# A residual block in fp32 on one core: bias added while VectorE empties the bank for tiles 18 to 27, four more warming products, and a new hand order

## The chip, the cores and the metric

The kernel runs on one core of a Trainium2 chip. The metric is device time in microseconds, the median of the runs shown. The engines are TensorE (PE, with its weight loads listed as PEld), VectorE (DVE), ScalarE (ACT), GpSimd (POOL) and SyncE (SP), whose queue issues nearly all DMAs. Matrix products write PSUM banks of 128 x 512 fp32; everything else lies in SBUF.

## The reference

Inputs are x (4, 1024, 512), cond (4, 256), W (1536, 512) and b (512), all fp32:

```python
hidden = jnp.concatenate([cond, cond], axis=-1)
x_mean = jnp.mean(x, axis=1, keepdims=True)
fused = jnp.concatenate([x, x_mean * ones_L, hidden[:, None, :] * ones_L], axis=-1)
out = x + jax.nn.relu(jnp.einsum('bld,do->blo', fused, W) + b)
```

So out = x + relu(x W0 + bias_r). W0 is the first third of W, and bias_r = mean_r W1 + hidden_r W2 + b is one row of 512 numbers for each of the four batch rows r.

## The kernel before, in words

**Tiles and products.** Batch and length give 32 tiles of 128 x 512; tiles 8r to 8r+7 belong to batch row r. fp32 is split: x and W0 are each cut into a high part (`hi`, `w_hi`, fp32r) and a low part (`lo`, `w_lo`), and a tile is 12 products 128x128 by 128x512: four blocks j of the contraction, times hi·w_hi (n=0), lo·w_hi (n=1) and hi·w_lo (n=2). A task `p5.3` issues all three n of tile 5, block 3; `p0.1.2` issues one. The 32 tiles have 384 products; tile 31 is done in two halves of 256 columns (`l` and `r`). The product is line 365.

**Getting x transposed.** x comes twice. For tiles 0 to 3 the plain rows (`X0.0` tile 0, `X0.1` tile 1, `X0.2` tiles 2 and 3) are regrouped (`y`, lines 236 and 238) and turned by TensorE (`T0` to `T2`, line 260). For the other tiles, in units of four (unit u holds tiles 4u-8 to 4u-5), a load with 512-byte pieces (`Z`) is turned by VectorE (`T`, line 262). ScalarE then makes `hi` and the row sums (`h`, line 269), and VectorE or GpSimd make `lo` (`l`, line 275; for odd j both inputs lie in SBUF, for even j one is a PSUM bank). Plain x is also loaded (`X`) for the residual.

**The bias row.** When all sums of a batch row r are there, GpSimd makes the mean (`to`), ScalarE puts the condition part into the bank `acc` (`as`), VectorE adds four terms (`m`, line 319), the halves are folded (`f`, `fa`), split (`vh`, `vl`, line 339), multiplied with ones on TensorE (`pb`, line 343), and ScalarE copies it out (`bc`, line 347). No tile of row r can get its bias before `bc`r.

**Emptying a bank.** Five banks `po` take the tiles in turn (tile t uses bank t mod 5, the left half of tile 31 bank 1, the right half bank 2). `WAYS` gives each tile one of three ways:

- K: ScalarE or VectorE copies the bank into a buffer `o` (`K`, lines 430 and 432); later GpSimd or VectorE add the bias (`b`, line 436), ScalarE or VectorE clip (`r`, lines 447 and 445), and GpSimd or VectorE add x (`F`, line 454).
- B: VectorE adds the bias while it empties the bank into `o` (`K`, line 440); then `r` and `F` as above.
- I: ScalarE writes the bias into the bank before the tile's first product (`P`, line 419; lines 399 and 403 for tile 31); the products add to it; VectorE clips and adds x in one instruction straight from the bank (`F`, line 423).

So tile t+5 may begin, in ways K and B, when `K`t is done; in way I it also waits for its own `P`, which waits for the emptying. There are 12 buffers `o`: the thirteenth tile that uses one waits for the `F` of the first.

**The order.** Nothing is scheduled automatically. `ORDER` (lines 22 to 49) is one list of task names, and each engine executes its own tasks strictly in that list's order; `@d`, `@a`, `@p` put a task on VectorE, ScalarE or GpSimd. A store `S` and the loads `X`, `Z`, `M`, `V`, `C`, `B` are issued in list order by SP, and a store waits in that queue for its `F`. `W0` and `W1` go through ScalarE's queue. `fill` (line 133) is a product of zeros (128x128 by 128x512 bf16) whose result nobody reads; there are seven, all before the first real product.

Of the kernel before, what the change touches and what calls it, by code (L numbers as in the profile page):

```python
# [19 lines left out]
ORDER = """
W0@a fill W1@a X0.0 X0.1 W2 fill relu fill W3 fill X0.2 fill Z3.3 fill y0.0@a T0.0 fill y1.0@d y1.1@p h0.0 y0.2@d
y0.1@p l0.0@d T0.2 T0.1 T1.0 T1.1 wh0r@a wh0l@d Z3.0 T1.2 T1.3 T0.3 h1.0 p0.0.1 h0.1 wh1@d C p1.0.0 h1.1 p0.0.0
l0.1@d h0.3 Z3.2 p1.1.0 wl1@p l1.0@d h0.2 p0.1.1 wh2@d Z3.1 h1.3 p0.1.0 l0.3@d h1.2 p1.0.1 l0.2@d p0.2.0 wh3@a
l1.1@d p1.2.0 wl2@d V p0.2.1 p0.3.0 wl3@p B p1.1.2 l1.2@d p0.3.1 Z4.2 y3.0@a y2.0@d p0.1.2 wl0r@d p1.2.2 p1.2.1
wl0l@p l1.3@d p1.1.1 T2.2 Z4.3 T2.3 p0.2.2 h2.3 T2.0 T2.1 h2.2 l2.3@d p1.3.2 h2.1 p1.3.0 l2.2@d Z4.1 p3.3 h2.0 Z4.0
l2.0@d p2.3 t0 l2.1@d p3.2 t3 p2.0 T3.3 p0.0.2 p0.3.2 T3.1 p3.0 h3.3 T3.0 K0@a p1.3.1 l3.3@p p2.1 t1 h3.0 T3.2 M2
p2.2 l3.0@d M1 h3.2 ac0@p p3.1 M3 h3.1 p1.0.2 p5.3 M0 K2@a K1@d to0 p4.3 Z5.3 l3.1@d ac1@p p5.0 Z5.0 t2 p4.0 l3.2@d
g0.0 p4.1 K3@d g0.1 Z5.2 d0.0 p6.3 p6.1 T4.3 Z5.1 d0.1 p4.2 T4.1 T4.0 p5.2 K4@a Z6.2 T4.2 as0 p7.1 g1.0 p5.1 Z6.0  # L30
h4.0 d1.0 p7.2 h4.3 l4.0@d p6.2 Z6.3 h4.2 m0.0 l4.3@p p7.0 K5@a m0.1 h4.1 p9.0 Z6.1 m0.2 g1.1 l4.1@p p6.0 m0.3 g2.0
Z7.2 p10.3 l4.2@d f0 d1.1 p7.3 fa0 Z7.1 p9.3 K7@a T5.2 d2.0 g2.1 p8.3 T5.0 Z7.0 vh0 p8.0 T5.1 d2.1 h5.0 p9.2 K6@d
h5.2 Z7.3 p8.2 T5.3 h5.1 vl0 p9.1 g3.1 X4.0 l5.1@p l5.2@d X1.0 p10.0 h5.3 l5.0@d p10.1 Z8.0 l5.3@p T6.0 p11.3 T6.2
Z8.1 to1 pb0 p8.1 T6.3 bc0@a T6.1 as1 p10.2 b0@p K9@a m1.0 p12.2 Z9.3 K8@a m1.1 p11.2 b1@p h6.0 m1.2 h6.3 p14.2 m1.3
h6.2 b3@p p12.1 r0@a l6.2@d p11.1 r1@a l6.0@d l6.3@p p13.2 K10@a h6.1 p11.0 f1 l6.1@p p15.3 r3@a fa1 p15.2 K11@a
T7.3 F1@p p15.1 vh1 T7.2 h7.3 p15.0 T7.0 F0@p h7.2 S1 p12.3 Z8.2 vl1 h7.0 p14.0 Z9.0 T7.1 F3@p Z8.3 p16.3 b2@d X5.0
h7.1 X4.1 pb1 p16.0 Z9.1 bc1@a to2 as2 p13.3 l7.3@p S0 K15 Z9.2 g3.0 p16.1 m2.0 b4@p X3.0 p13.1 m2.1 p14.3 m2.2 X1.1
b5@p r4@a p12.0 m2.3 p13.0 f2 X3.1 K12 l7.1@p r2@a p16.2 fa2 p14.1 K13 vh2 F4@p r5@a p17.3 vl2 p17.0 l7.0@d F2@p S4
T8.0 X2.1 pb2 p17.2 bc2@a d3.0 S2 P18 p17.1 K16 X5.1 h8.0 p18.1 T8.3 d3.1 P21 p18.0 T8.1 X2.0 K14 p18.2 h8.1 l7.2@d
p21.3 P19 X6.0 T8.2 h8.3 p21.1 l8.0@d as3 l8.3@p p19.0 S3 P20 T9.0 p19.1 h8.2 l8.1@p T9.3 p21.0 h9.0 l8.2@d h9.3  # L40
p18.3 F5@p T9.2 p20.3 T9.1 h9.2 p19.3 F18 S5 h9.1 p21.2 K17 P23 to3 p19.2 P22 b7@p m3.0 p20.2 r17@a m3.1 r12@a p22.1
b6@p m3.2 r16@a p23.3 m3.3 p22.3 l9.3@p F19 f3 p20.0 r7@a X7.0 fa3 p20.1 S19 r14@a X6.1 vh3 p23.0 F14@p vl3 p23.2
l9.2@d p23.1 F12@p b9@d pb3 p22.0 bc3@a F7@p r13@d P24 p22.2 F23 p24.0 F22 p24.3 F20 S22 P27 p24.2 S7 P28 r9@d S18
F21 p24.1 F9@p P25 S14 l9.0@d r6@a S20 p27.1 P26 F6@d F17@p p28.2 p27.3 b11@d b10@p S17 p26.3 S21 p26.0 l9.1@d S6
F13@p r10@a S9 p27.2 F24 p26.1 F16@p r11@d S24 p27.0 b8@d S23 p26.2 S12 F11@p X7.1 p28.3 F26 p25.0 S11 F27 P31l S26
P29 p25.1 S13 r15@a p25.2 P31r F15@p p29.2 p28.0 p25.3 p29.1 F25 p31.3r r8@d S25 P30 p29.3 F8@p S15 p31.2r S16
p31.0r S27 p30.1 F10@p S8 p28.1 p31.1r p29.0 F31r S31r p30.0 F29 S10 p31.3l F28 S29 p30.3 S28 p30.2 p31.0l F30
p31.2l p31.1l S30 F31l S31l
""".split()


# [437 lines left out]
```

## Time and profile before

| | |
|---|---|
| runs | 106.45 us median of 3 (105.53 to 107.67) |
| profiled execution | 106.27 us |
| its span, first to last instruction | 104.5 us |
| instructions | 1424 |
| PE / DVE / ACT / POOL busy | 97.6 / 79.1 / 59.1 / 70.1 us |
| data moved | 27.36 MB, 262 GB/s over the span |

All times inside the span are counted from its first instruction. The profiled execution's own time is 1.77 us longer than its span. "Idle before" in a row is the time that the engine waited just ahead of the instruction, and the name behind the arrow is what released it. Matmuls overlap their neighbours, so their durations do not add up; what counts is the distance from one start to the next.

### The profile page before, as it was taken

The numbers are of one execution on the slowest core, as the hardware profiler recorded it, in microseconds if no ns is written. First come the engines' busy times: TensorE is split into PE (matmuls) and PEld (weight loads), VectorE is DVE, ScalarE is ACT, GpSimd is POOL, SyncE is SP. The second block draws the span as 40 slices with busy tenths as digits, with TensorE's granted clock in tenths as the row PEclk, the third lists the DMA queues.
The fourth block names the chain that finished last, engine by engine and source line by source line (L and its number), as shares of the span: only waits on it lengthen the run. The fifth ranks groups of instructions, "written<-read, shape, count | busy, mean of one in ns | idle before, by whom it ended". The sixth has DMA issues, their size and how long they took to land.

```text
span 104.5 us, 1424 instructions
## 1 busy us (share of the span) xinstructions
PE 97.6 (93%) x423; PEld 76.6 (73%) x423; DVE 79.1 (76%) x129; ACT 59.1 (57%) x148; POOL 70.1 (67%) x69
## 2 busy tenths in 40 slices
...
GB/s 62 328 350 217 233 236 270 181 195 267 219 231 237 246 223 221 322 205 148 259 286 315 263 377 387 409 396 151 20 140 401 384 369 173 289 348 404 296 272 146
DMA packets 25345, 27.36 MB, mean 262 GB/s; under 512 B 1397, under 2 KB 15993, under 8 KB 25338
## 3 DMA queue, kind: packets, MB, share of 16 engines
...
q14 instruction: 4, 0.03, 0.1%
...
## 4 chain that ended last, share of the span: by engine, by line
PE 44%; DVE 22%; DMA 16%; ACT 7%; issue 4%; POOL 4%; SPq 1%; DVEq 0%; POOLq 0%
PE po L365 41%; DMA z<-in_x_dram 9%; DVE acc L319 6%; DMA x<-in_x_dram 4%; DVE xT L262 3%; DMA out_dram<-x 3%; DVE px L262 3%; DVE x L423 2%; DVE lo L275 2%; ACT po L419 2%; ACT hi L269 2%; DVE x L454 2%; DVE o L436 2%; ACT o L447 1%; POOL lo L275 1%
## 5 line engine op out<-in xcount | busy, mean ns | idle before, releaser
L365 PE MATMUL po<-w_hi,hi 128*128 128x512 f32 (+1 forms) x132 | 51.1, 393 | 1.5 <-ACT po L419 1.5
L365 PE MATMUL po<-w_hi,lo 128*128 128x512 f32 (+1 forms) x132 | 51.1, 389 | 0.0
L365 PE MATMUL po<-w_lo,hi 128*128 128x512 f32 (+1 forms) x132 | 50.1, 385 | 0.0
L365 PEld LDWEIGHTS po<-w_hi,hi 128*128 128x128 f32 x132 | 25.3, 192 | 8.2 <-ACT po L419 3.2
L365 PEld LDWEIGHTS po<-w_hi,lo 128*128 128x128 f32 x132 | 25.1, 190 | 5.2 <-DVE lo L275 0.4
L365 PEld LDWEIGHTS po<-w_lo,hi 128*128 128x128 f32 x132 | 24.8, 188 | 5.0
L454 POOL TENSOR_TENSOR x<-o,x 128x512 f32<-128x512 f32 x17 | 23.4, 1396 | 6.6 <-DVE o L445 4.5
L275 POOL TENSOR_TENSOR lo<-xT,hi 128x512 fp32r<-128x512 f32 x12 | 15.5, 1299 | 9.4 <-ACT hi L269 8.1
L319 DVE SCALAR_TENSOR_TENSOR acc<-w_mean,tot,acc 128x512 f32<-128x512 f32 x16 | 12.1, 754 | 1.1 <-DMA w_mean<-in_L_cond_W_dram 0.4
L275 DVE TENSOR_TENSOR lo<-px,hi 128x512 fp32r<-128x512 f32 (+2 forms) x20 | 11.5, 587 | 1.4 <-ACT hi L269 1.3
L269 ACT ACTIVATE hi<-px 128x512 fp32r<-128x512 f32 (+2 forms) x20 | 10.3, 521 | 3.8 <-PE px L260 2.1
L423 DVE SCALAR_TENSOR_TENSOR x<-po,x 128x512 f32<-128x512 f32 x13 | 8.5, 678 | 4.1 <-PE po L365 4.1
L262 DVE STREAM_TRANSPOSE xT<-z 128x512 f32<-128x512 f32 x14 | 9.3, 684 | 3.1 <-POOL cond L301 2.4
L269 ACT ACTIVATE hi<-xT 128x512 fp32r<-128x512 f32 x14 | 8.8, 631 | 3.8 <-DVE xT L262 3.8
L447 ACT ACTIVATE o<-o 128x512 f32<-128x512 f32 x14 | 8.3, 623 | 4.2 <-POOL o L436 4.2
L436 POOL TENSOR_TENSOR o<-o,bias 128x512 f32<-128x512 f32 x8 | 10.7, 1353 | 0.0
L419 ACT ACTIVATE po<-bias 128x512 f32<-128x512 f32 x13 | 7.5, 590 | 5.1 <-DVE x L423 5.0
L262 DVE STREAM_TRANSPOSE px<-z 128x512 f32<-128x512 f32 x14 | 9.4, 700 | 1.0 <-DMA z<-in_x_dram 0.6
L297 ACT ACTIVATE term<-wc,cT 128x512 f32<-128x512 f32 x8 | 5.6, 719 | 2.2 <-POOL tot L309 1.4
L301 POOL TENSOR_TENSOR cond<-b_sb,term 128x512 f32<-128x512 f32 x4 | 5.2, 1302 | 1.4 <-ACT term L297 1.4
L432 ACT ACTIVATE o<-po 128x512 f32<-128x512 f32 x9 | 5.2, 594 | 1.5 <-PE po L365 1.5
L301 POOL TENSOR_TENSOR cond<-cond,term 128x512 f32<-128x512 f32 x4 | 5.2, 1294 | 0.3
...
## 6 DMA issues: line engine op xcount, KB each, us to landing
...
```

Of the source, the lines that this page charges most:

```text
L262: nc.vector.transpose(xT.rearrange("p (n q e) -> p n q e", q=Q // E, e=E), zs[z_of(u)][:, : n * NQ].rearrange("p n (q j e) -> p n j q e", ...
L269: nc.scalar.activation(his[buf][:, col : col + m], xT, AF.Copy, accum_out=sums[:, r, j, s : s + 1])
L275: nc_of[e].tensor_tensor(los[buf][:, col : col + m], xT, his[buf][:, col : col + m].bitcast(F32), ALU.subtract)
L297: nc.scalar.activation(terms[k], wc[:, k], AF.Copy, scale=cT[:, k, r : r + 1])
L301: nc.gpsimd.tensor_tensor(conds[r % 2], conds[r % 2] if k else b_sb, terms[k], ALU.add)
L319: nc.vector.scalar_tensor_tensor(acc, w_mean[:, j, :], tot[:, r, j : j + 1], acc, ALU.mult, ALU.add)
L365: nc.tensor.matmul(v, lhsT=a[:, col : col + P], rhs=m, start=WAYS[t] != "I" and key not in done, stop=done.count(key) == 3 * J - 1, skip_g ...
L419: nc.scalar.activation(bank(t), biases[r], AF.Copy)
L423: nc.vector.scalar_tensor_tensor(x_tile(t), bank(t), 0.0, x_tile(t), ALU.max, ALU.add)
L436: nc_of[e].tensor_tensor(o, o, biases[r], ALU.add)
L447: nc.scalar.activation(o, o, AF.Relu)
L454: nc_of[e].tensor_tensor(x_tile(t), o, x_tile(t), ALU.add)
```

## The change

Three edits. `WAYS` turns tiles 18 to 27 from I to B, so that only tiles 28 to 31 keep I. `fill` writes bank `ps_o[2]` (first used by tile 2) where it wrote `acc` (used to turn tile 1). `ORDER` is written anew, with 11 `fill` where 7 were.

```diff
-WAYS = "KKKKKKKKKKKKBBBBBBIIIIIIIIIIIIII"
+WAYS = "KKKKKKKKKKKKBBBBBBBBBBBBBBBBIIII"
...
     def fill():
         nc.tensor.matmul(
-            acc, lhsT=warm, rhs=warm.rearrange("p (o d) -> p o d", o=1).to_broadcast([P, 4, P]),
+            ps_o[2], lhsT=warm, rhs=warm.rearrange("p (o d) -> p o d", o=1).to_broadcast([P, 4, P]),
             start=True, stop=True,
         )
```

Of `ORDER`, the beginning, the stretch around `pb2`, and the end, first as it was:

```diff
-W0@a fill W1@a X0.0 X0.1 W2 fill relu fill W3 fill X0.2 fill Z3.3 fill y0.0@a T0.0 fill y1.0@d y1.1@p h0.0 y0.2@d
-y0.1@p l0.0@d T0.2 T0.1 T1.0 T1.1 wh0r@a wh0l@d Z3.0 T1.2 T1.3 T0.3 h1.0 p0.0.1 h0.1 wh1@d C p1.0.0 h1.1 p0.0.0
-l0.1@d h0.3 Z3.2 p1.1.0 wl1@p l1.0@d h0.2 p0.1.1 wh2@d Z3.1 h1.3 p0.1.0 l0.3@d h1.2 p1.0.1 l0.2@d p0.2.0 wh3@a
-l1.1@d p1.2.0 wl2@d V p0.2.1 p0.3.0 wl3@p B p1.1.2 l1.2@d p0.3.1 Z4.2 y3.0@a y2.0@d p0.1.2 wl0r@d p1.2.2 p1.2.1
-wl0l@p l1.3@d p1.1.1 T2.2 Z4.3 T2.3 p0.2.2 h2.3 T2.0 T2.1 h2.2 l2.3@d p1.3.2 h2.1 p1.3.0 l2.2@d Z4.1 p3.3 h2.0 Z4.0
...
-b5@p r4@a p12.0 m2.3 p13.0 f2 X3.1 K12 l7.1@p r2@a p16.2 fa2 p14.1 K13 vh2 F4@p r5@a p17.3 vl2 p17.0 l7.0@d F2@p S4
-T8.0 X2.1 pb2 p17.2 bc2@a d3.0 S2 P18 p17.1 K16 X5.1 h8.0 p18.1 T8.3 d3.1 P21 p18.0 T8.1 X2.0 K14 p18.2 h8.1 l7.2@d
...
-F13@p r10@a S9 p27.2 F24 p26.1 F16@p r11@d S24 p27.0 b8@d S23 p26.2 S12 F11@p X7.1 p28.3 F26 p25.0 S11 F27 P31l S26
-P29 p25.1 S13 r15@a p25.2 P31r F15@p p29.2 p28.0 p25.3 p29.1 F25 p31.3r r8@d S25 P30 p29.3 F8@p S15 p31.2r S16
-p31.0r S27 p30.1 F10@p S8 p28.1 p31.1r p29.0 F31r S31r p30.0 F29 S10 p31.3l F28 S29 p30.3 S28 p30.2 p31.0l F30
-p31.2l p31.1l S30 F31l S31l
```

and as it is written:

```diff
+W0@a fill W1@a X0.0 X0.1 W2 fill relu fill W3 fill X0.2 fill Z3.1 fill y0.1@d y0.0@p y0.2@p fill T0.0 wh0r@d Z3.2
+T0.1 T0.2 wh0l@d h0.0 fill wl0r@p fill y1.0@d y1.1@a T0.3 l0.0@d fill h0.2 wl0l@p fill h0.1 T1.2 T1.0 p0.0.1 T1.1
+wh1@d Z3.3 T1.3 p0.0.0 h1.0 p0.0.2 Z3.0 h1.3 l1.0@d p1.0.2 wl1@p h1.2 l0.1@d p1.0.0 l1.3@d wh2@a p0.1.0 p1.0.1 wh3@d
+h1.1 p0.1.1 p0.2.0 h0.3 l0.2@d wl2@p C p1.2.0 l1.1@d p1.3.1 V p0.3.0 p1.1.0 B y3.0@d y2.0@a p1.3.0 p0.2.1 Z4.0
+l1.2@d p1.1.1 wl3@d p1.1.2 p0.2.2 T2.2 Z4.2 T2.3 p1.2.1 h2.2 T2.0 T2.1 l2.2@d p0.3.2 Z4.3 h2.0 p1.2.2 p3.2 h2.3
...
+l7.3@p T7.1 p17.0 b5@d h7.1 p19.3 b9@p h7.0 p17.3 r4@a l7.0@d p19.2 to2 g3.1 l7.2@d F4@p p16.2 r5@a m2.0 p18.3 K15
+b8@p S4 p18.2 Z9.1 m2.1 p16.3 X3.1 d3.1 m2.2 p19.0 m2.3 p18.1 F5@p T8.0 p16.1 f2 fa2 p20.3 b11@p S5 T8.3 S2 p17.2
+vh2 X3.0 h8.0 vl2 p17.1 F6@p X2.1 h8.3 S3 T8.2 p19.1 l7.1@d b7@p S6 p20.0 X4.0 pb2 S0 p18.0 bc2@a l8.3@p X7.0 h8.2
...
+p25.1 S9 r16@a vl3 p25.2 r19@a F16@p r23@d p26.0 l9.0@d p25.3 F19@p S16 pb3 X7.1 p26.3 bc3@a S17 F12@p P28 p27.1 K25
+p27.2 l9.2@d P30 F18@p p28.2 F14@d r25@a p30.2 l9.1@p K26 p28.0 S14 S18 F25@d P31l p27.0 S19 F23@p r26@a p30.0 K24
+S25 p31.2l F26@p S23 K27 p31.0l r24@a S12 p31.1l P29 p31.3l F20@p p30.3 P31r F31l F22@d S31l p29.1 S26 p28.1 S20
+r27@d S22 p29.0 F24@d F27@p p28.3 p29.3 F28 S24 p30.1 S27 S28 p29.2 F30 p31.1r F29 S30 p31.0r p31.3r S29 p31.2r F31r
+S31r
```

By task, with the engine that does it:

| task | before | after |
|---|---|---|
| `fill`, PE | 7 | 11 |
| `P`, ACT | 15 | 5 |
| `r`, ACT / DVE | 14 / 4 | 26 / 2 |
| `K`, DVE / ACT | 9 / 9 | 18 / 10 |
| `F` of way I, DVE (tile 31 has two) | 15 | 5 |
| `F` of ways K and B, POOL / DVE | 17 / 1 | 22 / 6 |
| `b`, POOL / DVE | 8 / 4 | 10 / 2 |
| `l`, POOL / DVE | 12 / 28 | 13 / 27 |

## Rows read from the trace of the kernel before

**Rows 1.** The page's first part: busy us (share of the span) x instructions.

```profile
PE 97.6 (93%) x423; PEld 76.6 (73%) x423; DVE 79.1 (76%) x129; ACT 59.1 (57%) x148; POOL 70.1 (67%) x69
```

**Rows 2.** Windows of 20 us: busy PE, PEld, DVE, ACT, POOL; then clock, DMA.

```profile
40.00:60.00 20.00, 19.77 (x87) 15.79 (x86) 19.36 (x30) 16.12 (x37) 19.62 (x20) 1.00 1.04 254
60.00:80.00 20.00, 19.91 (x85) 15.46 (x84) 17.97 (x27) 13.56 (x32) 14.02 (x13) 1.00 0.78 279
```

**Rows 3.** Timeline of PE, steady stretch: start us, us, what.

```profile
20.42 0.39 PE L365 MATMUL po<-w_hi,hi 128*128 128x512 f32 x1
...
29.48 0.39 PE L365 MATMUL po<-w_hi,lo 128*128 128x512 f32 x1
```

**Rows 4.** Timeline of PE, the start.

```profile
5.65 0.47 PE L260 MATMUL po<-term,o 128*128 128x128 f32 x1 [0.83 <-DVE o L238]
...
8.91 0.57 PE L365 MATMUL po<-w_hi,lo 128*128 128x512 f32 x1
9.32 0.39 PE L365 MATMUL po<-w_hi,hi 128*128 128x512 f32 x1
9.55 0.40 PE L365 MATMUL po<-w_hi,lo 128*128 128x512 f32 x1
...
12.12 0.66 PE L260 MATMUL px<-term,o 128*128 128x128 f32 x4
```

**Rows 5.** Timeline of VectorE and ScalarE, the start.

```profile
4.90 0.69 DVE L238 COPY o<-x 128x256 f32<-128x256 f32 x2 [3.65 <-DMA x<-in_x_dram]
...
7.40 0.43 DVE L219 CAST w_hi<-x 128x512 fp32r<-128x512 f32 x1 [1.40 <-DMA x<-in_L_cond_W_dram]
...
10.76 0.63 ACT L236 ACTIVATE o<-x 128x512 f32<-128x512 f32 x1 [1.51 <-DMA x<-in_x_dram]
```

**Rows 6.** Timeline of PE: three products about the waits of the later half.

```profile
57.37 0.39 PE L365 MATMUL po<-w_lo,hi 128*128 128x512 f32 x1
57.99 0.50 PE L343 MATMUL acc<-v_acc,ones 128*128 128x512 f32 x1 [0.23 <-DVE v_acc L339]
...
90.61 0.50 PE L365 MATMUL po<-w_hi,hi 128*128 128x512 f32 x1 [1.24 <-ACT po L419]
```

**Rows 7.** Timeline of VectorE and ScalarE ahead of 90.61 us.

```profile
88.94 1.27 DVE L423 SCALAR_TENSOR_TENSOR x<-po,x 128x512 f32<-128x512 f32 x2
89.65 0.39 ACT L399 ACTIVATE po<-bias 128x256 f32<-128x256 f32 x1 [4.25 <-DVE x L423]
89.97 0.58 ACT L419 ACTIVATE po<-bias 128x512 f32<-128x512 f32 x1
```

**Rows 8.** Groups by line and form: count, busy us, mean ns, idle before.

```profile
L454 POOL TENSOR_TENSOR x<-o,x 128x512 f32<-128x512 f32 x17 | 23.4, 1396 | 6.6 <-DVE o L445 4.5 <-ACT o L447 2.2
L275 POOL TENSOR_TENSOR lo<-xT,hi 128x512 fp32r<-128x512 f32 x12 | 15.5, 1299 | 9.4 <-ACT hi L269 8.1 <-DVE px L262 1.3
L436 POOL TENSOR_TENSOR o<-o,bias 128x512 f32<-128x512 f32 x8 | 10.7, 1353 | 0.0
L423 DVE SCALAR_TENSOR_TENSOR x<-po,x 128x512 f32<-128x512 f32 x13 | 8.5, 678 | 4.1 <-PE po L365 4.1
L447 ACT ACTIVATE o<-o 128x512 f32<-128x512 f32 x14 | 8.3, 623 | 4.2 <-POOL o L436 4.2
L436 DVE TENSOR_TENSOR o<-o,bias 128x512 f32<-128x512 f32 x4 | 4.9, 1229 | 0.0
L440 DVE TENSOR_TENSOR o<-po,bias 128x512 f32<-128x512 f32 x6 | 4.0, 674 | 0.2 <-POOL tot L309 0.2
...
L454 DVE TENSOR_TENSOR x<-o,x 128x512 f32<-128x512 f32 x1 | 1.8, 1844 | 0.1
```

**Rows 9.** Timeline of ScalarE: the copy of the first bias row.

```profile
39.20 0.60 ACT L347 ACTIVATE bias<-acc 128x512 f32<-128x512 f32 x1 [0.34 <-PE acc L343]
```

**Rows 10.** Timeline of VectorE: the last instruction.

```profile
101.37 0.42 DVE L403 SCALAR_TENSOR_TENSOR x<-po,x 128x256 f32<-128x256 f32 x1 [0.38 <-PE po L365]
```

**Rows 11.** The waits of PE's weight loads: us in total, times, longest us.

```profile
PEld po L365 <- ACT po L419: 3.2, 5, 1.7
```

More of the change, by code (lines that the diff above doesn't have):

```diff
@@ L27 @@
-wl0l@p l1.3@d p1.1.1 T2.2 Z4.3 T2.3 p0.2.2 h2.3 T2.0 T2.1 h2.2 l2.3@d p1.3.2 h2.1 p1.3.0 l2.2@d Z4.1 p3.3 h2.0 Z4.0
[L28 to L36, printed above, removed]
@@ L37 @@
-h7.1 X4.1 pb1 p16.0 Z9.1 bc1@a to2 as2 p13.3 l7.3@p S0 K15 Z9.2 g3.0 p16.1 m2.0 b4@p X3.0 p13.1 m2.1 p14.3 m2.2 X1.1
-b5@p r4@a p12.0 m2.3 p13.0 f2 X3.1 K12 l7.1@p r2@a p16.2 fa2 p14.1 K13 vh2 F4@p r5@a p17.3 vl2 p17.0 l7.0@d F2@p S4
-T8.0 X2.1 pb2 p17.2 bc2@a d3.0 S2 P18 p17.1 K16 X5.1 h8.0 p18.1 T8.3 d3.1 P21 p18.0 T8.1 X2.0 K14 p18.2 h8.1 l7.2@d
-p21.3 P19 X6.0 T8.2 h8.3 p21.1 l8.0@d as3 l8.3@p p19.0 S3 P20 T9.0 p19.1 h8.2 l8.1@p T9.3 p21.0 h9.0 l8.2@d h9.3
-p18.3 F5@p T9.2 p20.3 T9.1 h9.2 p19.3 F18 S5 h9.1 p21.2 K17 P23 to3 p19.2 P22 b7@p m3.0 p20.2 r17@a m3.1 r12@a p22.1
@@ L42 @@
-b6@p m3.2 r16@a p23.3 m3.3 p22.3 l9.3@p F19 f3 p20.0 r7@a X7.0 fa3 p20.1 S19 r14@a X6.1 vh3 p23.0 F14@p vl3 p23.2
-l9.2@d p23.1 F12@p b9@d pb3 p22.0 bc3@a F7@p r13@d P24 p22.2 F23 p24.0 F22 p24.3 F20 S22 P27 p24.2 S7 P28 r9@d S18
-F21 p24.1 F9@p P25 S14 l9.0@d r6@a S20 p27.1 P26 F6@d F17@p p28.2 p27.3 b11@d b10@p S17 p26.3 S21 p26.0 l9.1@d S6
-F13@p r10@a S9 p27.2 F24 p26.1 F16@p r11@d S24 p27.0 b8@d S23 p26.2 S12 F11@p X7.1 p28.3 F26 p25.0 S11 F27 P31l S26
-P29 p25.1 S13 r15@a p25.2 P31r F15@p p29.2 p28.0 p25.3 p29.1 F25 p31.3r r8@d S25 P30 p29.3 F8@p S15 p31.2r S16
@@ new lines @@
+l1.2@d p1.1.1 wl3@d p1.1.2 p0.2.2 T2.2 Z4.2 T2.3 p1.2.1 h2.2 T2.0 T2.1 l2.2@d p0.3.2 Z4.3 h2.0 p1.2.2 p3.2 h2.3
+l2.0@d h2.1 l2.3@d p2.0 l2.1@d Z4.1 l0.3@d p2.3 p2.2 T3.0 p3.1 T3.3 h3.0 T3.1 p3.0 h3.3 l3.0@d p2.1 h3.1 l3.3@p t3
+p3.3 T3.2 M1 K2@d p1.3.2 l3.1@p M0 p0.3.1 K1@a p4.0 t2 M2 h3.2 p0.1.2 ac0@p p6.0 M3 l3.2@d K0@a p4.3 Z5.2 t0 K3@d
+p5.3 t1 Z5.3 ac1@d g0.0 p7.2 p6.2 d0.0 Z5.0 g0.1 p5.2 d0.1 g1.0 p5.0 Z5.1 T4.1 T4.3 p5.1 d1.0 T4.2 p6.3 K5@a Z6.0
+T4.0 as0 p4.2 to0 g1.1 p7.3 Z6.3 h4.1 m0.0 p6.1 g2.0 l4.1@p m0.1 p4.1 Z6.2 h4.2 m0.2 p7.1 K4@a m0.3 h4.3 p7.0 Z6.1
```

10 lines of the change are left out of this document (added).

## Prediction, made before the changed kernel was run

> **What bounds the kernel now.** I read the page's shares first: PE 93% of the span, POOL 67%, DVE 76%, ACT 57% [rows 1]. A share of busy time is no rate, so next comes the distance between product starts: 40 steps from 20.42 to 29.48, 0.2265 us each [rows 3]. The kernel's 384 products (whole ones) need 87.0 us at that pace, and 87.0 us is most of the span. TensorE is the bound, and what can be won is time in which it stands or runs below that pace. There are two such places.
>
> The start: PE stands 0.83 us ahead of 5.65, since DVE sits 3.65 us on tile 1's `y1.0` while tile 0's `y0.2` is queued behind it [rows 4, 5]. The products then come at 0.41 us (8.91 to 9.32), and at 0.23 us only from 9.32 on [rows 4]. These are the two clock levels, 1.2 and 2.4 GHz, over 512 columns, though the clock column of this profile prints 1.00 from the start. When tile 2's turning begins at 12.12, only 17 products are issued.
>
> The later half: from product 210 (57.37) to product 340 (90.61) lie 132 steps with `pb2` and `pb3`, which is 29.9 us at full pace, against 33.24. So 3.3 us are lost [rows 3, 6]. The largest part is the wait ahead of 90.61: ScalarE has `P29` queued behind `P31l`, and `P31l` waits 4.25 us until VectorE has done `F26` (88.94, the first of two), though tile 29's own bank had been emptied earlier [rows 7]. PE's weight loads wait 3.2 us for such bias writes in all, five times [rows 11]. One of them is `P18` behind `bc2`, one `P24` behind `bc3`: in way I the first product of a batch row needs the row's bias. `pb2` itself waits for `vl2` on DVE [rows 6].
>
> **The change, part by part.** The sums go against the profiled execution, 106.27 us (span 104.5 and 1.77 around it); the median of the runs is 0.18 above it.
>
> *Start.* Tile 0's four blocks are now regrouped by POOL and DVE ahead of tile 1's, so `T0.1` and `T0.2` no longer stand behind X0.1's landing at 4.90 [rows 5]. The four added `fill` stand around `T0.3`, where PE stood idle before. At the low level's 0.43 us each (512 columns at 1.2 GHz; 0.41 traced) they are 1.7 us of PE time, laid over 0.83 us of waiting and the time that the earlier transposes win. Counting 0.43 per 512 columns from the first instruction on, the first real product comes at about 7.0, as now, so their cost is hidden. Without that cover they would cost 0.9 (1.7 less the 0.83 of waiting). After five products comes `p0.1.0`, which needs W1 (landed at 7.40, [rows 5]) and 0.43 us of `wh1`: 7.9. If the clock is up by then, 13 products at 0.2265 end at 10.9, and then X0.2 decides: `y2.0` starts at its landing, 10.76, and takes 0.63 [rows 5]. Tile 2 is turned from 11.45 on, after 18 products, where it was 12.12 after 17. The gain is 0.67 + 0.23 = 0.9 us. Ends: nothing won if the low level lasts until 9.3 as it does now (the same count then gives 12.35 after 18, no gain), and a loss of 0.9 if the four `fill` are not covered at all; 0.9 won at best, as X0.2's landing doesn't move. I take 0.9, since the engines that feed PE are free at that time.
>
> A rule speaks against this gain. The Trainium skill, "TensorE: Matmul & The Clock Gate", Part 4, says that transposes do not count as PE activity in the way that products do, and Part 1 that the state without sustained activity is the throttled one. The trace has transposes, pauses and a few products ahead of the rise at 9.32, which fits the rule but doesn't single it out. By that rule the transposes between the warming products could leave the rise where it is, and the start would win nothing (a rival below).
>
> *Tiles 18 to 27 by way B.* Removed: ten `P` on ACT, and the waits of the first products for them. The DVE instruction at the bank stays one and costs the same, 674 ns against 678 [rows 8]. So the bank is free one ACT hop earlier, a batch row's bias is needed when its first tile ends instead of when it begins, and `P31l` has no `P` but P29 and P31r behind it. Of the 3.3 us I let 2.3 go and keep 1.0. The ends: 3.3 if all go; nothing if DVE is late everywhere. DVE decides, because it idles only 2.7 us of the 40 from 40 to 80 [rows 2] and its work hardly changes: nine more `K` (+6.1), ten fewer `F` from the bank (-6.8), two `b` fewer (-2.5), two `r` fewer (taken as 0.7 each, -1.4), and five more `F` from buffers, between 0.67 (two inputs, one in a bank) and 1.84 (both in SBUF, the one traced) each [rows 8]. That is -1.2 to +4.6 us, and I take +1.6, with 1.23 each as in DVE's L436, which was executed four times. But DVE's work is better placed. `pb2` comes 33 products later in the list (after 243, not 210), 7.5 us, and DVE has 5.8 us more ahead of it: F0, ac1 and b5 at 1.23, K14 and four transposes or `lo` at about 0.68, less K6 and one `lo`. That leaves 1.7 us, of which PE's earlier arrival takes 0.9. The wait for `vl2` goes, but not by much, and that is why I keep 1.0. What is late next is a `K` on DVE: K21 stands three products behind tile 20's, nine ahead of the first product that needs its bank.
>
> *What is added.* Twelve `r` on ACT at 0.623, less ten `P` [rows 8], on an engine that is 57% busy [rows 1]: nothing, as long as the `b` ahead of each `r` is in time. ACT works in order, so an `r` that waits for POOL holds the `h` behind it. `r7`, `r8` and `r11` stand between `h8.3` and `h9.0`, and PE needs `h9.0` only over 60 products later.
>
> POOL gets five more `F`, two more `b`, and one `lo`: 7.0 + 2.7 + 1.3 = 11 us. From `bc0` on it has 58.7 us: 10 `b` at 1.353, 8 `lo` at 1.299, 22 `F` at 1.396 [rows 8], two `d` (taken as `lo`) and three `to` (taken as 0.5). `bc0` follows `pb0`, which now stands after 120 products instead of 129; so it ends at 39.80 - 9 x 0.2265 - 0.9 = 36.9 [rows 3, 9]. POOL's last `F`, `F27`, can't end before 95.6. It needs idle time on top: 0.4 us in the twenty from 40 to 60, when it was behind, and 6.0 in the twenty from 60 to 80, when it waited for others [rows 2]. With the longer queue I take 2.0. `F27` ends at 97.6.
>
> A rule of the Trainium skill bears here: "SBUF — State Buffer", section "SBUF: two separate sides", says that DVE with two SBUF inputs and GpSimd exclude each other for a whole instruction. The 1.84 us of the one `F` on DVE, against 0.67 with one input in a bank, agrees [rows 8]. By that rule the five added `F` on DVE would each hold POOL for some 0.7 us too, an estimate of 3.5 us and a time of 107.4, which lies within the first rival below.
>
> *The sum.* PE's path: 104.5 - 0.9 - 2.3 = 101.3. POOL's path: SP issues S27, S28, S30, S29 and S31r in this order; with 0.45 for each step after `F27`, S31r goes out 1.8 us after 97.6, and from there to the end it is 2.7, as from the end of the last `F` now (101.79 to 104.5) [rows 10]. That gives 102.1, and the later path decides. 102.1 + 1.77 = 103.9 us. X7.1, the load of tiles 30 and 31, also stands behind S16 and so behind POOL's `F16`; if POOL is late, `F31l` on DVE waits for it, with three more `F` behind it.
>
> **The rivals.**
>
> 1. *POOL becomes the bound.* For it: 58.7 us of work in the 60 that are left, in order, with an `r` on another engine between each `b` and its `F`. Against it: in 40 to 60 it ran at 98% [rows 2]. The end follows `F27` + 4.5 as soon as `F27` ends after 96.8. With 7 us idle, a little more than it had in 40 to 80, it is 58.7 + 36.9 + 7 = 102.6, span 107.1, time 108.9: slower. From 102.3 on, the time is more than 2% above the median.
> 2. *DVE keeps its late places.* All 3.3 us of waiting come back under other names, and only the start wins: 105.4. For it: DVE is 97% busy in 40 to 60 [rows 2], and the room at `pb2` is 0.8 us. Against it: the longest wait was one of order on ACT, and that order is gone.
> 3. *The clock doesn't rise earlier.* Nothing is won at the start, PE and POOL are both 0.9 later: 104.8. For it, the seven `fill` of now did not raise the clock, and the rows show it raised only behind transposes and the first products [rows 4]; against it, PE would hardly pause any more between the first `fill` and the first product.
>
> **How the numbers follow.** Chances: the forecast 0.50, POOL 0.18, DVE 0.20, the clock 0.12. A difference of 2% (to 104.3 or from 108.6) is about what a measurement of this kernel can tell from no change. Faster by over 2%: 0.43 of the forecast's 0.50, 0.07 of the clock's, 0.03 of DVE's and 0.02 of POOL's, together 0.55. Slower: 0.08, all POOL's. The rest, 0.37, is within 2%. The forecast's own range is 102.2 (PE keeps 0.1 of the 1.0 us, POOL idles 0.3) to 104.9. To hold 8 in 10 the range reaches up past DVE's 105.4 and into POOL's middle: 102.1 to 106.4.
>
> **What would show it.** The start is right if product starts are 0.23 apart before 8.5 and tile 2 is turned near 11.5. The later half is right if no weight load waits for L419 between `pb2` and the last four tiles, and if DVE's L440 has 16 instructions near 674 ns. POOL's part is right if POOL is over 90% busy from 40 to 95 and `F27` ends near 97.6. The forecast is wrong if POOL waits several times for ACT's `r`, if a `K` on DVE ends after PE has stopped, or if the stores behind S27 wait in SP's queue beyond 99.

## The result, and the profile after

The changed kernel takes 102.72 us, median of 4 runs (102.19 to 104.16), against 106.35 us of the kernel before in the same comparison (4 runs, 105.53 to 107.67): ratio 0.9667, 95% interval [0.958, 0.9754]. It is faster by 3.3%. The prediction, 103.9 (102.1 to 106.4) and faster as the likeliest, held. A median here is over all runs of a kernel, while a ratio leaves disturbed executions out, so a median can lie above what its ratio says.

The profiled execution took 102.85 us, its span 101.1 us. Lines from 134 on have moved by one: the product is L366, `F` on GpSimd L455, `K` of way B L441, `l` L276, `b` L437, `r` L446 (DVE) and L448 (ACT). First the page's busy shares and the windows that answer to [rows 1, 2].

```profile
PE 95.8 (95%) x427; PEld 76.4 (76%) x427; DVE 79.3 (78%) x129; ACT 60.6 (60%) x150; POOL 80.0 (79%) x77
...
40.00:60.00 20.00, 20.00 (x90) 16.43 (x89) 18.44 (x28) 12.67 (x30) 19.91 (x18) 1.00 1.16 233
60.00:80.00 20.00, 20.00 (x89) 16.21 (x88) 17.09 (x26) 14.90 (x35) 19.57 (x18) 1.00 1.04 356
```

By its busy column PE is never idle from 40 to 80. POOL, which had 6.0 us of idle time from 60 to 80, now has 0.43, while DVE has a little more room than before. PE's start, as in [rows 4], with a weight load behind it and DVE's `wh1`:

```profile
5.47 0.59 PE L134 MATMUL po<-warm 128*128 128x512 bf16 x2
...
7.88 0.63 PE L366 MATMUL po<-w_hi,lo 128*128 128x512 f32 x2
8.35 0.63 PE L366 MATMUL po<-w_hi,hi 128*128 128x512 f32 x2
9.10 0.50 PE L366 MATMUL po<-w_hi,lo 128*128 128x512 f32 x1
...
11.04 0.60 PE L261 MATMUL px<-term,o 128*128 128x128 f32 x4
...
9.09 0.19 PEld L366 LDWEIGHTS po<-w_hi,lo 128*128 128x128 f32 x1 [0.56 <-DVE w_hi L220]
...
6.95 0.43 DVE L220 CAST w_hi<-x 128x512 fp32r<-128x512 f32 x1 [1.04 <-DMA x<-in_L_cond_W_dram]
```

Two products that together take 0.63 us are 0.23 apart, and the pairs start 0.47 apart: full pace, 2.4 GHz by the spacing, from the warming pair at 5.47 on. Tile 2 is turned at 11.04 after 18 products; before it was 12.12 after 17. W1 had landed at 6.95, not 7.40 as in [rows 5], and PE once waited 0.56 us for `wh3` (9.09). The later half has two pauses left:

```profile
75.05 0.39 PE L366 MATMUL po<-w_lo,hi 128*128 128x512 f32 x1
75.42 0.50 PE L366 MATMUL po<-w_hi,hi 128*128 128x512 f32 x1
...
84.69 0.39 PE L366 MATMUL po<-w_hi,hi 128*128 128x512 f32 x1
85.43 0.50 PE L366 MATMUL po<-w_hi,lo 128*128 128x512 f32 x1 [0.36 <-DVE lo L276]
...
96.95 0.28 PE L366 MATMUL po<-w_lo,hi 128*128 128x256 f32 x1
```

With the steps of 0.33 behind them they cost about 0.9 us over the pace of [rows 3]. The last product starts at 96.95; before it was 101.06, so PE is 4.1 us earlier. The waits of the weight loads name other engines than in [rows 11]; no bias write of ScalarE is among them:

```profile
PEld po L366 <- DVE lo L276: 0.8, 1, 0.8
...
PEld po L366 <- DVE o L441: 0.6, 2, 0.4
```

DVE's rows around the two pauses show what was late, and its last row is the last `F`:

```profile
74.08 1.29 DVE L441 TENSOR_TENSOR o<-po,bias 128x512 f32<-128x512 f32 x2 [1.19 <-POOL x L455]
...
82.12 1.47 DVE L446 TENSOR_SCALAR o<-o 128x512 f32<-128x512 f32 x1
...
84.11 0.67 DVE L441 TENSOR_TENSOR o<-po,bias 128x512 f32<-128x512 f32 x1
84.70 0.67 DVE L276 TENSOR_TENSOR lo<-px,hi 128x512 fp32r<-128x512 f32 x1
...
97.27 0.42 DVE L404 SCALAR_TENSOR_TENSOR x<-po,x 128x256 f32<-128x256 f32 x1 [0.74 <-PE po L366]
```

At 74.08 DVE empties the bank of tile 20 into the buffer `o` that tile 8 had, and waited 1.19 us until GpSimd had done `F8`. That is a chain from POOL over a buffer, DVE and a bank to PE: an engine off PE's direct inputs sets when PE may go on. At 84.70 it is DVE's own queue: `r23` (1.47 us) stands ahead of `l9.2`, whose product waits.

POOL's first `b` behind `bc0`, and its last `F`, `F27`; then the groups that answer to [rows 8]:

```profile
36.56 1.30 POOL L437 TENSOR_TENSOR o<-o,bias 128x512 f32<-128x512 f32 x1
...
93.95 1.67 POOL L455 TENSOR_TENSOR x<-o,x 128x512 f32<-128x512 f32 x1 [0.36 <-DVE o L446]
```

```profile
L455 POOL TENSOR_TENSOR x<-o,x 128x512 f32<-128x512 f32 x22 | 30.0, 1385 | 0.7 <-DVE o L446 0.4
...
L441 DVE TENSOR_TENSOR o<-po,bias 128x512 f32<-128x512 f32 x16 | 10.5, 679 | 1.6 <-POOL x L455 1.4
...
L455 DVE TENSOR_TENSOR x<-o,x 128x512 f32<-128x512 f32 x6 | 7.2, 1194 | 0.0
```

From 36.56 to 95.62 POOL waited for others 0.7 us in all. `S27` goes out at 95.65, right behind `F27`, and S28, S30 and S29 follow 0.43 to 0.49 us apart; SP is free at 97.51, `F31r` ends at 97.69 and S31r leaves at 97.72. The two paths meet within 0.2 us, PE's the later. SP's waits say the same from its side: stores stood 11.8 us behind GpSimd's `F` in nine waits, and the last store of all took longer to land than before (1.2 us of waiting then).

```profile
SPq L148 <- POOL x L455: 11.8, 9, 3.6
...
SPq L486 <- DMA out_dram<-x: 1.9, 1, 1.9
```

### The profile page after: what moved, and what is told of

It is laid out like the page before. It is cut to its first block, busy times and chain, and to the rows that moved or that the text cites. A ratio compares the mean times of both kernels' runs of the same rounds, so it can differ in the third digit from the quotient of the medians.

```text
span 101.1 us, 1437 instructions
## 1 busy us (share of the span) xinstructions
PE 95.8 (95%) x427; PEld 76.4 (76%) x427; DVE 79.3 (78%) x129; ACT 60.6 (60%) x150; POOL 80.0 (79%) x77
## 3 DMA queue, kind: packets, MB, share of 16 engines
q1 hardware_dynamic: 25050, 26.75, 102.6%
## 4 chain that ended last, share of the span: by engine, by line
PE 38%; DMA 23%; POOL 18%; DVE 10%; ACT 4%; issue 2%; ACTq 1%; SPq 1%; POOLq 0%
PE po L366 37%; DMA z<-in_x_dram 9%; POOL x L455 8%; DMA x<-in_x_dram 8%; DMA x<-in_L_cond_W_dram 6%; POOL lo L276 4%; POOL o L437 4%; DVE acc L320 2%; DVE lo L276 2%; ACT hi L270 2%; DVE w_hi L220 1%; DVE o L446 1%; POOL cond L302 1%; DVE o L441 1%; PE px L261 1%
## 5 line engine op out<-in xcount | busy, mean ns | idle before, releaser
L366 PE MATMUL po<-w_hi,lo 128*128 128x512 f32 (+1 forms) x132 | 50.7, 387 | 0.5 <-DVE lo L276 0.4
L366 PE MATMUL po<-w_hi,hi 128*128 128x512 f32 (+1 forms) x132 | 50.2, 385 | 0.0
L366 PE MATMUL po<-w_lo,hi 128*128 128x512 f32 (+1 forms) x132 | 50.1, 385 | 0.0
L455 POOL TENSOR_TENSOR x<-o,x 128x512 f32<-128x512 f32 x22 | 30.0, 1385 | 0.7 <-DVE o L446 0.4
L366 PEld LDWEIGHTS po<-w_hi,lo 128*128 128x128 f32 x132 | 24.8, 188 | 6.1 <-DVE lo L276 0.8
L366 PEld LDWEIGHTS po<-w_hi,hi 128*128 128x128 f32 x132 | 24.8, 188 | 5.4 <-DVE o L441 0.6
L366 PEld LDWEIGHTS po<-w_lo,hi 128*128 128x128 f32 x132 | 24.7, 188 | 5.0 <-ACT hi L270 0.3
L276 POOL TENSOR_TENSOR lo<-xT,hi 128x512 fp32r<-128x512 f32 x13 | 17.7, 1367 | 9.2 <-ACT hi L270 9.2
L448 ACT ACTIVATE o<-o 128x512 f32<-128x512 f32 x26 | 15.2, 622 | 4.0 <-DVE o L441 3.4
L437 POOL TENSOR_TENSOR o<-o,bias 128x512 f32<-128x512 f32 x10 | 13.9, 1390 | 0.0
L276 DVE TENSOR_TENSOR lo<-px,hi 128x512 fp32r<-128x512 f32 (+2 forms) x20 | 11.5, 588 | 2.2 <-ACT hi L270 2.2
L441 DVE TENSOR_TENSOR o<-po,bias 128x512 f32<-128x512 f32 x16 | 10.5, 679 | 1.6 <-POOL x L455 1.4
L455 DVE TENSOR_TENSOR x<-o,x 128x512 f32<-128x512 f32 x6 | 7.2, 1194 | 0.0
L433 ACT ACTIVATE o<-po 128x512 f32<-128x512 f32 x10 | 5.9, 590 | 0.8 <-PE po L366 0.8
L224 POOL TENSOR_TENSOR w_lo<-x,w_hi 128x256 fp32r<-128x256 f32 (+1 forms) x4 | 4.2, 1068 | 1.8 <-DVE w_hi L220 1.8
```

Of the source, the lines that this page charges most:

```text
L276: nc_of[e].tensor_tensor(los[buf][:, col : col + m], xT, his[buf][:, col : col + m].bitcast(F32), ALU.subtract)
L366: nc.tensor.matmul(v, lhsT=a[:, col : col + P], rhs=m, start=WAYS[t] != "I" and key not in done, stop=done.count(key) == 3 * J - 1, skip_g ...
L433: nc.scalar.activation(o, bank(t), AF.Copy)
L437: nc_of[e].tensor_tensor(o, o, biases[r], ALU.add)
L441: nc.vector.tensor_tensor(o, bank(t), biases[r], ALU.add)
L448: nc.scalar.activation(o, o, AF.Relu)
```

## The experiments

The theory at the outset was that the gain has two halves that add up, the start and the order of the work at the late banks, and that POOL is now level with PE at the end. Against it stood: that a gain in one place is eaten in the other; that the added warming products make the start; that way B as such makes the later half; and that POOL, off PE's path, can lose time without harm. Kernels that begin with `h_` are halves, those with `a_` start from the changed kernel, those with `b_` from the one before. Several shift line numbers by one or two.

**The start alone.** The new order up to and with `T2.1`, with 11 `fill` in the free bank; from there the old order and the old ways.

```diff
-W0@a fill W1@a X0.0 X0.1 W2 fill relu fill W3 fill X0.2 fill Z3.3 fill y0.0@a T0.0 fill y1.0@d y1.1@p h0.0 y0.2@d
+W0@a fill W1@a X0.0 X0.1 W2 fill relu fill W3 fill X0.2 fill Z3.1 fill y0.1@d y0.0@p y0.2@p fill T0.0 wh0r@d Z3.2
...
```

> The new order up to and with T2.1 (11 fill, in the free bank), then everything else in the old order with the old ways. Theory A, what the start wins reaches the end: tile 2 is turned near 11.1 instead of 12.12 us and the last product starts some 1.3 us earlier, time about 105.0. Rival B, the old rest is bound by VectorE and by the bias writes, so PE only waits longer there: tile 2 near 11.1 too, but the product behind P29 still starts within 0.4 us of 90.6, time 106.0 to 106.4.

104.22 us (104.0 to 104.46), ratio 0.9859 [0.9788, 0.993], span 102.6. Tile 2 is turned at 11.47. The pause that was 1.63 us in the kernel before ([rows 6]) is there as it was, 1.59:

```profile
88.75 0.50 PE L364 MATMUL po<-w_hi,hi 128*128 128x512 f32 x1 [1.21 <-ACT po L418]
```

The last product starts at 99.19, 1.9 us earlier than before: 0.65 at tile 2, one product (0.23) more by then, and some 1.0 in smaller pauses further on, as at `pb2` (0.44 from one start to the next in place of the 0.62 of [rows 6]). So the start's gain reaches the end, as theory A has it; nothing later eats it.

**The rest alone.** The old order through `T2.1` with its seven `fill`, then the new order and the new ways.

> The old start up to and with T2.1 (7 fill), then everything else in the new order with the new ways. Theory A, PE's path: the new rest keeps its pace, everything comes 1.3 us later than in the changed kernel, time about 104.0. Rival B, the new rest is bound by GpSimd's and VectorE's queues, which do not start with PE: they take up the late start, time 102.7 to 103.1, with PE's gaps of 75 and 85 us gone.

104.88 us (103.79 to 106.37), too scattered for a ratio. In its profile (103.79, span 102.0) tile 2 is turned at 12.08, the last product starts at 97.89 (0.95 later than with the new start) and `F27` ends at 96.57. The late start is carried through to both ends, as A has it.

**Warming products: seven, and none.** The changed kernel without the four `fill` behind `T0.0`, and without any `fill` (their results are read by nobody).

```diff
-T0.1 T0.2 wh0l@d h0.0 fill wl0r@p fill y1.0@d y1.1@a T0.3 l0.0@d fill h0.2 wl0l@p fill h0.1 T1.2 T1.0 p0.0.1 T1.1
+T0.1 T0.2 wh0l@d h0.0 wl0r@p y1.0@d y1.1@a T0.3 l0.0@d h0.2 wl0l@p h0.1 T1.2 T1.0 p0.0.1 T1.1
```

> The changed kernel without the four fill that stand behind T0.0; nothing else differs. Theory A, the four fill bring the clock up: without them products come 0.41 to 0.43 us apart until 8 us or later, tile 2 is turned at 12 to 12.4 instead of 11.04, time 103.7 to 104.0. Rival B, regrouping tile 0 first was what mattered: the rise moves by less than 1 us, tile 2 by less than 0.4, time 102.7 to 103.0.

Seven: 104.38 us (102.25 to 106.93), ratio 0.9678 [0.9568, 0.9788]; tile 2 at 11.07, last product at 96.34, products at full pace by 7.8. The rival's numbers: in this execution the four weren't needed.

> The changed kernel without any of its 11 fill. Theory A, the warming products bring the clock up: without them products come 0.43 us apart until 9 us or later, tile 2 is turned at 12 us or later instead of 11.04, time up by 0.9 or more, 103.6 and over. Rival B, the real products and transposes bring it up soon enough and the start is bound by its loads: tile 2 by 11.4, time 102.5 to 103.1.

None: 102.92 us (102.72 to 105.64), ratio 0.9725 [0.9655, 0.9795]. PE's timeline:

```profile
7.06 1.05 PE L365 MATMUL po<-w_lo,hi 128*128 128x512 f32 x2
7.91 1.03 PE L365 MATMUL po<-w_hi,hi 128*128 128x512 f32 x2
8.76 0.66 PE L365 MATMUL po<-w_hi,lo 128*128 128x512 f32 x2
9.26 0.63 PE L365 MATMUL po<-w_hi,hi 128*128 128x512 f32 x2
...
11.57 0.60 PE L260 MATMUL px<-term,o 128*128 128x128 f32 x4
```

Pairs 0.85 apart until 8.76 are products at 0.43, the lower level of 1.2 GHz. It costs 0.5 us at tile 2 (11.57 against 11.04), and nothing at the last product (96.83 against 96.95). This lies between the two theories. The three ratios (11, seven, none) overlap, each by 0.7 to 1.1% to either side, so what the warming products are worth is not shown; it is less than the 1 us or so that these runs can tell.

**One task moved.** The kernel before with `P29` ahead of `P31l` in ScalarE's queue; nothing else.

```diff
-F13@p r10@a S9 p27.2 F24 p26.1 F16@p r11@d S24 p27.0 b8@d S23 p26.2 S12 F11@p X7.1 p28.3 F26 p25.0 S11 F27 P31l S26
-P29 p25.1 S13 ...
+F13@p r10@a S9 p27.2 F24 p26.1 F16@p r11@d S24 p27.0 b8@d S23 p26.2 S12 F11@p X7.1 p28.3 F26 p25.0 S11 F27 P29 P31l
+S26 p25.1 S13 ...
```

> The kernel before with one task moved: P29 is queued on ScalarE ahead of P31l instead of behind it. Theory A, the wait of 1.6 us at 90.6 is one of order on ScalarE: it goes nearly whole, time about 104.9. Rival B, VectorE is late for tile 29 anyway or the next product waits in its place: less than 0.5 us is won, time 105.9 or more.

105.28 us (103.95 to 106.1), ratio 0.9864 [0.974, 0.9988]. ScalarE's and PE's timelines:

```profile
85.72 0.60 ACT L418 ACTIVATE po<-bias 128x512 f32<-128x512 f32 x1 [0.52 <-DVE x L422]
...
88.86 0.39 ACT L398 ACTIVATE po<-bias 128x256 f32<-128x256 f32 x1 [2.54 <-DVE x L422]
...
8.12 0.40 PE L364 MATMUL po<-w_hi,lo 128*128 128x512 f32 x1
8.35 0.39 PE L364 MATMUL po<-w_hi,hi 128*128 128x512 f32 x1
...
9.47 0.47 PE L364 MATMUL po<-w_hi,hi 128*128 128x512 f32 x1 [0.50 <-DVE w_hi L218]
```

`P29` now goes at 85.72 and `P31l` still waits its 2.54 us, with nothing urgent behind it. PE's pause at 90.6 is gone and its last product starts at 98.72, 2.3 us earlier; 1.4 of these are that pause, 0.2 the earlier tile 2 (11.95), and the rest smaller pauses that this execution hasn't. So a wait of order was worth some 1.4% by itself, without way B, though the interval (0.1 to 2.6%) leaves its size open. The start shows a second thing: with the old order, products came at full pace from 8.12, and still tile 2 was turned only 0.17 earlier, since PE then waited for `wh2` (9.47), which took 1.35 us on DVE in place of the 0.43 of `wh1`, beside GpSimd's `wl1`. In the old order an earlier rise of the clock alone won almost nothing.

**Way B in the old order.** Tiles 18, 24 and 27 by way B, their `o` in spare room, `r` on ScalarE, `F` on GpSimd, `P29` ahead of `P31l`. At first with `r27` ahead of `P29`:

```diff
-WAYS = "KKKKKKKKKKKKBBBBBBIIIIIIIIIIIIII"
+WAYS = "KKKKKKKKKKKKBBBBBBBIIIIIBIIBIIII"
...
-        o = parks[park_of[t]]
+        o = wc[:, int(t == 24)] if t in (18, 24, 27) else parks[park_of[t]]
```

> The kernel before with P29 queued ahead of P31l, and tiles 18, 24 and 27 by way B (their buffers o lie in wc, their r on ScalarE, their F on GpSimd); order and start else as before. Theory A, the first products of these three tiles wait for their bias writes only: against the kernel with P29 moved alone, PE's gaps at about 59.5, 76 and 79 us go and 0.8 to 1.0 us are won, time about 1.4 + 0.9 below the kernel before, 104.0. Rival B, the banks are emptied late by VectorE or GpSimd's three added F (4.2 us) come in the way: less than 0.3 us against P29 moved alone.

107.95 us (106.31 to 108.39), ratio 1.0116 [0.999, 1.0243]. The pauses before tiles 18, 24 and 27 went, but the order brought the old fault back: `r27` waited 3.10 us for `K27`, with `P29` behind it.

```profile
89.35 0.63 ACT L446 ACTIVATE wc<-wc 128x512 f32<-128x512 f32 x1 [3.10 <-DVE wc L439]
89.88 0.58 ACT L418 ACTIVATE po<-bias 128x512 f32<-128x512 f32 x1
...
90.52 0.79 PE L364 MATMUL po<-w_hi,hi 128*128 128x512 f32 x1 [2.38 <-ACT po L418]
```

Behind that pause of 2.8 us products came 0.43 apart from 91.1 to 93.7. In a second version `P29` stands behind `r24`, and `r27` behind `P31r`.

> Tiles 18, 24 and 27 by way B in the old order again, with P29 queued directly behind r24 and r27 behind P31r, so that no r which waits for a K stands ahead of P29. Theory A, what spoiled the first try was r27 ahead of P29 on ScalarE: PE's wait of 2.8 us near 88 is gone, and against P29 moved alone 0.5 to 1.0 us are won, time about 104.0 to 104.5. Rival B, the three added F on GpSimd or VectorE's late emptying take the place: PE still waits over 1 us between 85 and 92, time 105.3 or more.

106.94 us (105.31 to 107.33), ratio 1.004 [0.9986, 1.0094]. PE has no pause between 85 and 92, as theory A has it, and its last product starts at 98.46, earlier than with `P29` moved alone (98.72); and yet the kernel gains nothing. `F31l` ends at 99.19, but its store leaves only at 100.42. `S24` stood in SP's queue for 3.7 us until GpSimd had done `F24`, at 89.45 (with `P29` moved alone, VectorE had done it at 85.69), and the 17 DMAs behind it followed one another closely to the end. That store took 3.4 us to land, against 1.7 with `P29` moved alone. DVE's `F31l`, and SP's waits from 64 us on:

```profile
98.77 0.42 DVE L402 SCALAR_TENSOR_TENSOR x<-po,x 128x256 f32<-128x256 f32 x1 [0.38 <-PE po L364]
...
SPq L146 <- POOL x L453: 5.1, 3, 3.7
```

So way B for these three tiles, in the old order, is no gain; it hands work to POOL, and an order has to be found in which POOL's queue and SP's bear it. The way and the order can't be told apart in the other direction: in the new order tile 18 begins 33 products ahead of `pb2`, and with way I it would need a bias that isn't there.

**POOL loaded.** The changed kernel with one addition of 128 x 512 more on GpSimd behind `F8`, whose result nobody reads.

```diff
+    @task("extra")
+    def _(e):
+        nc.gpsimd.tensor_tensor(conds[0], conds[0], b_sb, ALU.add)
...
-F8@p F9@d
+F8@p extra F9@d
```

> The changed kernel with one added GpSimd addition of 128x512 (1.3 us, on buffers that nobody reads any more) behind F8. Theory A, GpSimd's path is level with PE's at the end (0.2 us behind it): F27 ends 1.3 us later, near 96.9, the stores behind it too, time up by 1.0 to 1.3, about 103.8. Rival B, PE alone sets the end and GpSimd has room: less than 0.4 us, time 102.6 to 103.1.

104.86 us (102.83 to 108.04), ratio 0.9758 [0.9658, 0.9858]. The profile is of an execution of 108.04 us and settles nothing (one row of it stands in the last section). The same kernel again, beside the changed kernel itself:

> The changed kernel with one added GpSimd addition behind F8, once more, beside the unchanged one. Theory A, GpSimd's path is level with PE's: F27 ends 1.3 us later than in the unchanged kernel, time up by 1.0 to 1.3. Rival B, PE alone sets the end: less than 0.4 us.

104.11 us (103.28 to 105.87), ratio 0.9821 [0.9753, 0.9888].

```profile
76.24 2.34 DVE L319 SCALAR_TENSOR_TENSOR acc<-w_mean,tot,acc 128x512 f32<-128x512 f32 x3 [1.70 <-POOL tot L310]
...
79.22 0.50 PE L369 MATMUL po<-w_hi,hi 128*128 128x512 f32 x1 [0.66 <-DVE o L444]
...
94.37 1.67 POOL L458 TENSOR_TENSOR x<-o,x 128x512 f32<-128x512 f32 x1 [0.36 <-DVE o L449]
```

> The changed kernel itself, beside the three others on one chip. If the time at which the clock rises and X0.2 lands varies from one execution to the next, tile 2 is turned within 0.6 us of 11.04 and F27 ends within 0.6 us of 95.6; the ratio lies in the first measurement's interval, 0.958 to 0.975.

The changed kernel: 102.36 us (102.15 to 106.76), ratio 0.9659 [0.9599, 0.9718]; its `m3.0` and `F27` in the same rows:

```profile
75.10 2.34 DVE L320 SCALAR_TENSOR_TENSOR acc<-w_mean,tot,acc 128x512 f32<-128x512 f32 x3 [0.43 <-POOL tot L311]
...
93.27 1.68 POOL L455 TENSOR_TENSOR x<-o,x 128x512 f32<-128x512 f32 x1 [0.36 <-DVE o L446]
```

`F27` ends 1.09 us later with the extra addition (96.04 against 94.95), the last product starts 1.08 later (97.35 against 96.27), the span is 1.1 longer, and the ratios differ by 0.016, some 1.7 us. 1.3 us on POOL comes out at the end nearly whole, and on PE too, by the bias row: `m3.0` on DVE waits 1.70 us in place of 0.43 for `to3`, which GpSimd now does 1.1 us later; `K22` stands behind `m3.2` in DVE's queue; and PE's start at 79.22, the first that needs `K22`'s bank, comes 1.04 us behind the one before. POOL has no room left: theory A. `F27` itself came 0.67 us earlier here than in the first profile, a little more than expected of two executions.

**`r23` and `r27` on ScalarE**, since `r23` held `l9.2` on DVE.

```diff
-r19@a F16@p r23@d
+r19@a F16@p r23@a
...
-r27@d S22
+r27@a S22
```

> The changed kernel with r23 and r27 on ScalarE (0.62 us each) instead of VectorE (1.49 each beside GpSimd's work). Theory A, r23 on VectorE is what makes l9.2, and so PE at 84.7 us, late, and r27 is what F27 waits 0.36 us for: PE's gap of 0.75 us closes, F27 ends 0.4 us earlier, time down by 0.4 to 0.7, about 102.1. Rival B, the paths of GpSimd and SP hold the end where it is: less than 0.2 us.

103.37 us (101.55 to 107.93), too scattered for a ratio; in its profile the pause near 85 is gone, and others stand at 50.5 and 90.

> The changed kernel with r23 and r27 on ScalarE once more, now beside the unchanged one. Theory A, VectorE's 1.49 us for r23 is what PE waits for near 85 us: no wait of PE there, and 0.4 to 0.7 us less than the changed kernel. Rival B, GpSimd's queue holds the end: less than 0.2 us.

103.73 us (102.05 to 106.26), ratio 0.9638 [0.9561, 0.9714] against 0.9659 of the changed kernel beside it: no difference. The profile again has no pause near 85, but there W1 landed 1.04 us later than in the first profile, tile 2 was turned at 12.09, and any gain is drowned:

```profile
7.99 0.43 DVE L219 CAST w_hi<-x 128x512 fp32r<-128x512 f32 x1 [1.75 <-DMA x<-in_L_cond_W_dram]
```

None of these versions beats the changed kernel by more than can be measured.

## Why the prediction was right, and where its numbers were not

*What bounds.* TensorE with two places of loss: right. The new start alone gives 1.4% (0.7 to 2.1), the moved `P29` alone 1.4% (0.1 to 2.6). Added up these are 2.8 of the 3.3%, but no run has the two together without way B.

*The start, 0.9 us.* It was 1.08 for tile 2 and one product more, 1.3 in all. The failing step is "and then X0.2 decides". In no execution of the new start did tile 2 wait for X0.2: `y2.0` began anywhere from 8.91 to 11.05, and PE turned tile 2 each time straight behind its products. Two other things set the time, whichever came later:

| | first product | `wh1` starts | tile 2 is turned |
|---|---|---|---|
| seven `fill` | 5.69 | 6.99 | 11.07 |
| the changed kernel | 6.04 | 6.95 | 11.04 |
| `r` on ScalarE, first run | 6.43 | 7.44 | 11.52 |
| extra addition, first run | 6.37 | 7.72 | 11.82 |
| `r` on ScalarE, second run | 6.29 | 7.99 | 12.09 |
| extra addition, second run | 6.25 | 6.45 | 10.83 |
| the changed kernel, second run | 6.41 | 6.76 | 11.00 |
| the start alone | 6.87 | 6.20 | 11.47 |

In the upper five tile 2 is turned 4.08 to 4.10 behind `wh1`, and so behind W1's landing. The wait is that of the eleventh product, `p1.3.1`, for `wh3` (9.09), a wait that the sum doesn't have: `wh3` on DVE took 1.15 us beside GpSimd's `wl1`, which `wh1` releases. In the start alone POOL stood idle then, and `wh3` took 0.42 us. The changed kernel's `wh3` and `wl1` (with `wl2`), then the `wh3` of the start alone:

```profile
7.89 1.15 DVE L220 CAST w_hi<-x 128x512 fp32r<-128x512 f32 x1
...
7.46 2.73 POOL L224 TENSOR_TENSOR w_lo<-x,w_hi 128x512 fp32r<-128x512 f32 x2 [1.17 <-DVE w_hi L220]
...
8.62 0.42 DVE L218 CAST w_hi<-x 128x512 fp32r<-128x512 f32 x1
```

In the lower three no product waited, and tile 2 is turned 4.58 to 4.60 behind the first product. The start alone had the earliest W1 and still not the earliest tile 2: its last four `fill` ran at the lower level, 0.43 for each, and the transpose behind them started at 6.62 (5.90 in the changed kernel).

At the 7.40 of the kernel before, the upper rows give 11.5, 0.6 less than its 12.12; with the product more that is the 0.9 forecast. The size is right there by luck, since the wait is another. The other 0.4 is W1's earlier landing in this execution. These are landings that came as they came; no run moved that load, `wl1` or `wh3`.

That the fill raises the clock, another premise of the sum, is not settled. In the new start full pace began between 3.9 and 6.8 us in the seven executions with 11 `fill`, at 4.3 in the one with seven, at 8.8 in the one with none; in the old start, with seven, anywhere from 4.2 to 9.3. With none the clock cost 0.5 us at tile 2 and nothing visible at the end. With the old order it made little difference whether the products came at full pace from 9.3 or from 8.1. What is left as the cause of the start's gain is its new order as a whole, tile 0 regrouped ahead of tile 1 and the casts in other places; no run took it apart.

The rule of the Trainium skill in "TensorE: Matmul & The Clock Gate", Part 4, on transposes stood beside the third rival. The runs neither bear it out nor refute it: the pace rose at different times behind the same instructions.

*Way B, 2.3 of 3.3 us go.* PE gained 4.1 in all, 1.3 at the start, so 2.8 behind it, smaller pauses elsewhere included; 0.9 is left where 1.0 was kept. The prediction had the cause of the largest wait right (order on ScalarE), and the wait that takes its place as well (a `K` on DVE), but it took K21 by its place in DVE's list; what came late was K20, by the buffer that `F8` on POOL still held. No weight load waits for L420, `K` of way B has 16 instructions of 679 ns, DVE is 0.2 us busier, not 1.6.

*POOL.* The bound "can't end before 95.6", which has no idle time in it, is where `F27` ended (95.62), by luck: `bc0` ended at 36.1, not 36.9, in part since the start gained more, and POOL waited 0.7 us. With the 2.0 us of idle time that the forecast took, 97.6 was forecast, so `F27` came 2.0 earlier, and POOL's path was not the later one by 0.8 but level with PE's.

*The tail, 2.7 us.* It was 3.4 from the end of the last `F` to the end of the span. The last stores are released one after the other behind `F27`, and the last of all landed 2.4 us after its issue, not 1.7. That is the term that lies against the others: the span is 101.1, and 102.1 was forecast.

*The rivals.* POOL as the bound came half true: no slower kernel, but an engine without room, as the extra addition showed. DVE's late places fell: in the twenty from 60 to 80 it idles 2.9 us where it had 2.0. The Trainium skill's rule in "SBUF — State Buffer", section "SBUF: two separate sides", would have cost 3.5 us by the estimate. The trace agrees with the rule, at a lower price. From `bc0` on, an addition or subtraction of 128 x 512 on GpSimd took 1.28 to 1.31 us, but 1.49 to 1.77 us in the nine cases in which a DVE instruction on SBUF (`F`, `b`, `l` or `r`) was running when it began. And a DVE `F` that began while GpSimd was at work took 0.99 to 1.72 us. So whichever began first went through, and the other paid. `F22` on DVE, which began behind POOL's `F26` (90.61), and `F24`, which began ahead of POOL's `F27` (93.95, 1.67 us):

```profile
90.71 1.72 DVE L455 TENSOR_TENSOR x<-o,x 128x512 f32<-128x512 f32 x1
...
93.79 0.68 DVE L455 TENSOR_TENSOR x<-o,x 128x512 f32<-128x512 f32 x1
```

The nine cost POOL 3.8 us, where five cost it 2.2 us in the kernel before: 1.6 us more. `F8`, for which `K20` waited, and `F27` are two of them. The mean of POOL's `F` hides it (1385 ns after, 1396 before), since five of 22 were longer after and four of 17 before.
